# A decoder block on one Trainium2 core: accumulated values kept in the queries' tile, one group's sums moved to VectorE, one feed-forward's activations moved to ScalarE

## The chip, the cores and the metric

The kernel runs on one core of one Trainium2 chip. The metric is the device time of one launch, in microseconds (us). Before the change three runs gave 2163.33, 2163.65 and 2166.55 us, so the median is 2163.65 us.

The engines are named as the profile names them: PE is TensorE (PEld is its weight loads), DVE is VectorE, ACT is ScalarE, POOL is GpSimd, SP is SyncE, which issues most DMAs.

## The reference, cut to what matters

Four sequences of 1024 tokens and 512 features pass a self-attention with gates (phase 0), a cross-attention to a context of 384 features (phase 1), and a small feed-forward, each behind a layer norm and with a residual. Both attentions have 16 heads of 32. All data are 32-bit floats.

```python
q = (query @ Wq + bq).reshape(B, Nq, H, D).transpose(0, 2, 1, 3)
attn = softmax(q @ k^T * scale)            # cross-attention
x = x + (attn @ v) @ Wo + bo
s = layernorm(x) @ Win + bin_              # feed-forward: M = 64 units
h = relu(s[..., None] * W1 + b1)           # INNER = 16 activations per unit
g = sum_h(h * W2) + b2
out = x + g @ Wout + bout
```

What the change touches is in the cross-attention and the feed-forward: the softmax's denominator (a sum of exponentials over the keys), the division of attn @ v by it, and the 16 relus.

## The kernel before, in words

**Units and steps.** The work is eight *units*, (phase, sequence), in the list `order`; units 0 to 3 are the self-attention, 4 to 7 the cross-attention. Unit 7 is the *last unit*. A unit has two *halves* of 512 queries (`hf`), a half has four *groups* of four heads (`g`), and a group has eight *steps*, one per tile of 128 keys (`kt`). In one step of `attention(u, hf)`:

- `scores(g, kt)` (L615) multiplies keys and queries on PE (L623) into two PSUM tiles of two heads each, and ACT takes the exponential of each (L629) into a tile `e`. Six tiles `e` exist, three steps' worth. The PSUM tiles `s` are two; in the last unit, when no other work needs them (`spare`), the two banks `f` serve as a third (`score_banks`, L108).
- One step later `times` (L668) multiplies the values with `e` into the PSUM tile `av` (L671).

**The denominators.** Two ways are used. Where `shared` is false (units 4 to 6), DVE adds the exponentials of all four heads over the keys, two additions of 128x1024 per step (L646, L648). Where `shared` is true (phase 0 and the last unit), DVE adds those of the first two heads only, one addition per step, and PE sums the other two by multiplying with a column of ones (L679), four matmuls in every second step.

**The end of a group.** In the first step of the next group `normalize` (L685) copies `av` from PSUM with ACT into a tile `both` (L688) and, where `shared`, the sums `sm` too (L690). `both` has one buffer of three slots. One step later `add_up` (L698) sums the DVE partial sums over the partitions with a column of ones (L701), ACT copies that out (L702), and SP carries the sums through DRAM to a layout of 128x16 (L707 to L719). `divide` (L722) takes the reciprocals, and SP carries them through DRAM to all rows of a tile `recb` (L741, L745). `multiply` (L750) multiplies `both`'s first slot with `recb` into the queries' own tile `q` (L751), whose group is no longer needed as queries. `after(steps, f, behind)` holds such a part back by a number of steps; it then comes ahead of that step's scores, or behind them with `behind`. In the last unit the division is three steps after the sums, and the multiplication three steps after the division, ahead of the scores; in other units it is two steps, behind the scores.

**What runs beside.** `beside(u, hf)` lists what is put between the steps of a half, and `run` spreads it over them by its load. In the last unit that is, for the half before: the output projection (`project`, L106 called at L837), its residual and statistics on DVE (L845 to L850), the norm (L319) into tiles `r2` (two buffers), rows written to DRAM and read back turned (L323, L328), 32x32 transposes on DVE (L334), the feed-forward's first product (L937), the 16 hidden activations one by one (`hidden`, L982), and the output product into two PSUM banks `f` (L1011) with the residual on DVE (L1019). The hidden activations of a half are left over to the next half. Activation h is a relu with a scale and a bias per partition; the next call adds it, weighted, to `g` on DVE (L1000). The relu is on DVE (L989) for halves of units before the last, on ACT (L993) for the last unit's first half. Tile `hid` has two buffers, so activation h waits for the addition of activation h-2.

**Order.** The program writes each engine's instructions in the order of these calls, and each engine takes them in that order. The group that ends the kernel (`closing`) has its own sums and division (`settle`, L775).

Of the kernel before, what the change touches and what calls it, by code (L numbers as in the profile page):

```python
# [10 lines left out]
F32 = mybir.dt.float32  # L11
U32 = mybir.dt.uint32
AF = mybir.ActivationFunctionType
ALU = mybir.AluOpType
AX = mybir.AxisListType

P = 128
# [51 lines left out]
def moderate_path(tc: tile.TileContext, a: dict, out: bass.AP, flag: bass.AP):  # L69
    nc = tc.nc  # L70
    x = a["x"]
    with ExitStack() as st:
# [108 lines left out]
            raw.append(wp.tile([P, NC, D], F32, tag="w", name="w"))  # L181
            nc.sync.dma_start(raw[0], a["attn_Wout"].rearrange("(c p) f -> p c f", p=P))

        rot = p2.tile([P, NC, P], F32, tag="r2", name="rot")

        cs = p1.tile([P, 2, NC], F32, name="cs")
        gain = p1.tile([P, NC], F32, name="gain")
# [173 lines left out]
        def after(steps, f, behind=False):  # L361

            soon.append((tick[0] + steps, behind, f))
# [236 lines left out]
        def attention(u, hf):  # L600
# [3 lines left out]
            steps = []  # L604
            sums = 2 if ph == 0 else 1

            shared = ph == 0 or u + 1 == len(order)

            def apart(g):
                return 2 if u + 1 < len(order) else 3  # L610
# [1 line left out]
            def closing(g):  # L612
                return (u, hf, g) == (len(order) - 1, 1, HG - 1)

            def scores(g, kt):  # L615
                q, k = me["q", hf], me["k"]
                es = []
                for i in range(2):
                    two, reads = score_banks(not (closing(g) and kt == NT - 1))
                    for j in range(2):  # L620
                        r = slice((2 * i + j) * DH, (2 * i + j + 1) * DH)
                        for m in range(0, P, 64):
                            nc.tensor.matmul(  # L623
                                two[j][m : m + 64], lhsT=k[r, g, kt * P + m : kt * P + m + 64], rhs=q[r, g, :],
                                start=True, stop=True,
                            )
                    e = p4.tile([P, 2, HALF], F32, tag="e", name="e", bufs=6)
                    for h, s in reads:
                        nc.scalar.activation(e[:, h, :] if len(reads) == 1 else e[:, h.start, :], s, AF.Exp, scale=SCALE)  # L629
                    es.append(e)  # L630
                me["e", kt] = es
                if closing(g):
                    if kt == 0:
                        me["first"] = [p1.tile([P, 2, HALF], F32, tag=f"es{i}", name="es") for i in range(2)]
                    if kt in (0, 4, NT - 1):
                        return es
                    to = me["first"] if kt < 4 else me["rest"]
                    for i in range(2):
                        nc.vector.tensor_tensor(to[i], me["e", kt - 1][i] if kt % 4 == 1 else to[i], es[i], ALU.add)
                    if kt == 3:  # L640
                        after(2, lambda: by_ones(me["first"], True, False), behind=True)
                    return es
                for i in range(1 if shared else 2):
                    if kt == 1:
                        me.setdefault("es", {})[i] = p1.tile([P, 2, HALF], F32, tag=f"es{i}", name="es")
                        nc.vector.tensor_tensor(me["es"][i], me["e", 0][i], es[i], ALU.add)  # L646
                    elif kt > 1:
                        nc.vector.tensor_tensor(me["es"][i], me["es"][i], es[i], ALU.add)  # L648
                if ph == 0 and kt > 0:
                    if kt == 1:  # L650
                        me["eg"] = p1.tile([P, 2, HALF], F32, tag="es1", name="eg")
                    for h in range(2):
                        eg, gate = me["eg"][:, h, :], lambda t: me["sw"][:, t, HG * g + h, 1:2]
                        if kt == 1:
                            nc.scalar.activation(eg, me["e", 0][0][:, h, :], AF.Identity, scale=gate(0))  # L655
                        nc.vector.scalar_tensor_tensor(eg, es[0][:, h, :], gate(kt), eg, ALU.mult, ALU.add)  # L656
                return es
# [10 lines left out]
            def times(g, kt, es):  # L668
                for h in range(HG):
                    r = slice(h * DH, (h + 1) * DH)  # L670
                    nc.tensor.matmul(  # L671
                        av[r, :], lhsT=me["v"][:, kt, HG * g + h, :], rhs=es[h // 2][:, h % 2, :],
                        start=(kt == 0), stop=(kt == NT - 1),
                    )
                if shared and kt % 2 and not closing(g):

                    for j in range(4):
                        t, h = kt - 1 + j // 2, j % 2
                        nc.tensor.matmul(  # L679
                            sm[j * DH : j * DH + sums, :],  # L680
                            lhsT=me["sw"][:, t, HG * g + 2 + h, :] if ph == 0 else ones, rhs=me["e", t][1][:, h, :],
                            start=(kt == 1), stop=(kt == NT - 1),
                        )

            def normalize(g):  # L685
                i = (u * 2 + hf) * HG + g
                both = p1.tile([P, 3, HALF], F32, tag="both", name="both")
                nc.scalar.copy(both[:, 0, :], av)  # L688
                if shared:
                    nc.scalar.copy(both[:, 1, :], sm)  # L690
                    added = [me["es"][0][:, 0, :], me["es"][0][:, 1, :]]
                    if ph == 0:
                        added += [me["eg"][:, 0, :], me["eg"][:, 1, :]]
                else:
                    added = [me["es"][h // 2][:, h % 2, :] for h in range(HG)]
                after(1, lambda: add_up(g, i, both, added), behind=True)

            def add_up(g, i, both, added):  # L698

                for j, e in enumerate(added):  # L700
                    nc.tensor.matmul(sm[j * DH : j * DH + 1, :], lhsT=ones, rhs=e, start=True, stop=True)  # L701
                nc.scalar.copy(both[:, 2, :], sm)  # L702

                c, s1, s2 = cs_[i % 2], sum1_d[i % 4], sum2_d[i % 4]
                rows = both.rearrange("(j r) s q -> j r s q", r=DH)
                n = len(added)
                nc.sync.dma_start(s1[0:n], rows[0:n, 0, 2, :])  # L707
                if not shared:
                    nc.sync.dma_start(c[:, 0, 0, :], s1[0:n].rearrange("h (q e) -> (h q) e", e=INNER))
                else:  # L710
                    for k in range(sums):
                        nc.sync.dma_start(s2[k], rows[:, k, 1, :])
                    nc.sync.dma_start(
                        c[0:64, 0:sums, 0, :], s1[0:n].rearrange("(s h) (q e) -> (h q) s e", h=2, e=INNER)
                    )
                    for k in range(sums):
                        nc.sync.dma_start(
                            c[64:, k, :, :], s2[k].rearrange("(p h) (q e) -> (h q) p e", h=2, e=INNER)
                        )  # L719
                after(apart(g), lambda: divide(g, i, both, c))  # L720

            def divide(g, i, both, c):  # L722
                if shared:
                    both_ = p2.tile([P, sums, INNER], F32, tag="c2", name="both_")
                    nc.vector.tensor_tensor(both_, c[:, 0:sums, 0, :], c[:, 0:sums, 1, :], ALU.add)
                else:
                    both_ = c[:, 0:1, 0, :]
# [16 lines left out]
                for j in range(HG):  # L744
                    nc.sync.dma_start(  # L745
                        all_[j * DH : (j + 1) * DH, :], rec_d[i % 4][j : j + 1, :].to_broadcast([DH, HALF])
                    )
                after(apart(g), lambda: multiply(g, both, all_), behind=u + 1 < len(order))

            def multiply(g, both, all_):  # L750
                nc.vector.tensor_tensor(me["q", hf][:, g, :], both[:, 0, :], all_, ALU.mult)  # L751
                me["divided", hf] = g

            def step(g, kt):
# [20 lines left out]
        def settle(u, hf, g):  # L775
# [1 line left out]
            me = S[u]  # L777
            i = (u * 2 + hf) * HG + g
            rec = p1.tile([P, HALF], F32, tag="recb", name="recb")
            den = p1.tile([P, 3, HALF], F32, tag="both", name="den")[:, 0, :]  # L780
            few = p2.tile([P, INNER], F32, tag="rec", name="few")
            column = den.rearrange("p (b j) -> p b j", j=NB)[:, :, 0]

# [17 lines left out]
        def post(u, hf):  # L801
# [24 lines left out]
            def project(t):  # L826
                def part(cs, to=None):
                    def f():
# [20 lines left out]
                        nc.vector.bn_stats(s6, r)  # L849
                        nc.vector.bn_aggr(res["mv"][:, t, :], s6)  # L850
                        if ph == 0:
                            r2 = p2.tile([P, D], F32, tag="r2", name="r2")
                            nc.gpsimd.tensor_tensor(r2, r, bo_bc, ALU.add)  # L853
                            nc.sync.dma_start(x1b_d[b][4 * hf + t], r2)
                    return len(cs), f
# [45 lines left out]
            def norm(t):  # L901
                def f():
                    if last:
# [5 lines left out]
                        else:  # L909
                            normalized(to, res[t], res["mv"], res["rs", t], t)  # L910
                        return
                    r2 = p2.tile([P, 1, D], F32, tag="r2", name="r2")
                    normalized(r2[:, 0, :], res[t], res["mv"], res["rs", t], t)
                    away(rows_d[b][hf], r2, t, 1)
                return [(0, f)]
# [47 lines left out]

            def products():
                hid = res["hids"]
                both = p1.tile([P, 3, HALF], F32, tag="both", name="g")
                part, g = both[:, 0, 0 : 2 * P], both[:, 1, 0 : 2 * P]
                ph_ = bank()[:, 0 : 2 * P]
                on_pe = sorted(res["diag"], key=lambda h: (h - BY_ACT) * 1.25 if h >= BY_ACT else h * 1.6 + 0.5)
# [12 lines left out]
            def hidden(h):  # L982
                def f():

                    own = u + 1 < n
                    if h < INNER:
                        hid = p2.tile([P, 2 * P], F32, tag="hid", name="hid")
                    if own and h < INNER:
# [880 lines left out]
```

## Time and profile before

| what | value |
|---|---|
| runs | 2163.33, 2163.65, 2166.55 us; median 2163.65 us |
| profiled execution | 2166.25 us, of which the span from first to last instruction is 2164.4 us |
| instructions | 52976 |
| mean granted PE clock | 0.998 |
| last unit's first half, groups 0 to 3 start at | 1916.24, 1939.89, 1972.88, 1993.95 us |
| last unit's second half, groups 0 to 3 start at | 2018.08, 2042.58, 2075.57, 2096.64 us |
| ACT L629, exponential of 128x1024 | 1023 ns each |
| DVE L648, addition of 128x1024 | 1227 ns each |
| DVE L989 and ACT L993, relu of 128x256 | 409 ns and 605 ns each |
| DVE L751, the multiplication of 128x512 | 686 ns each |

A matmul of 32-bit floats appears as two records in the trace, so four matmuls side by side are eight. Four records on the four column groups of the array take about 0.43 us to issue; a record's own duration (592 ns) contains the drain, which overlaps what follows. A step's length is therefore read from the start of one step's scores to the start of the next. In the profile's tables "idle before" is the idle time of an engine just before an instruction, and the arrow names what ended it. "PEclk" is the granted share of PE's full clock.

### The profile page before, as it was taken

The page shows a single profiled execution, that of the slowest core. Times are in us where ns is not written, and L with a number is a line of the kernel's source. Part 1 is how long each engine was busy: PE and PEld are TensorE (multiplying, and loading weights), DVE is VectorE, ACT ScalarE, POOL GpSimd, SP SyncE. Part 2 cuts the span into 40 slices and gives each one's busy share as a digit, 9 for nine tenths or more (in the row PEclk, how much of TensorE's full clock was granted, in tenths as well). Part 3 has the DMA queues.
Part 4 walks back from the last instruction along what each step waited for, and adds up shares of the span by engine and source line. Part 5 has one row for each costly group of instructions (what it writes and reads, how often), then busy time and mean ns, then how long its engine had stood idle before and what let it go on. Part 6 is the DMA issues. An engine that isn't in the chain of part 4 may idle for free.

```text
span 2164.4 us, 52976 instructions
## 1 busy us (share of the span) xinstructions
PE 2145.8 (99%) x22792; PEld 555.9 (26%) x22792; DVE 1503.4 (69%) x2251; ACT 1233.1 (57%) x1495; POOL 133.0 (6%) x182
## 2 busy tenths in 40 slices
PE   9999999999999999999999999999999999999998
PEld 4322222222222222222222222222222222222223
DVE  3477675786766866657667666787878868876656
ACT  0156545655556554565666666565655566566765
POOL 2000010040120100001000010000000000000001
PEclk9999999999999999999999999999999999999999
DMA  6412134032331221211322113322423122322231
GB/s 169 122 47 68 52 100 114 19 87 69 90 109 34 81 59 53 68 48 65 71 71 79 63 59 69 96 66 71 89 80 102 63 61 57 98 60 71 71 90 47
DMA packets 154136, 161.71 MB, mean 75 GB/s; under 512 B 47002, under 2 KB 92698, under 8 KB 152740
## 3 DMA queue, kind: packets, MB, share of 16 engines
q1 hardware_dynamic: 149828, 156.14, 25.9%
q8 instruction: 180, 2.95, 0.6%
q0 software_dynamic: 2080, 0.98, 0.3%
q10 hardware_dynamic: 1984, 1.12, 0.2%
q14 instruction: 64, 0.52, 0.1%
HBM read 115.40 MB, written 42.74 MB: 73 GB/s over the span
## 4 chain that ended last, share of the span: by engine, by line
PE 97%; DVE 1%; ACT 1%; issue 1%; DMA 0%; SPq 0%; POOL 0%; DVEq 0%; ACTq 0%
PE f L106 37%; PE s L623 24%; PE av L671 23%; PE sm L679 6%; PE sm L701 3%; PE s L106 1%; PE f L937 1%; ACT e L629 1%; PE f L623 0%; PE f L1011 0%; DMA xin<-in_x 0%; PE f L498 0%; DVE res L1019 0%; PE f L971 0%; DVE es L648 0%
## 5 line engine op out<-in xcount | busy, mean ns | idle before, releaser
L629 ACT ACTIVATE e<-s 128x1024 f32<-128x1024 f32 x997 | 969.4, 1023 | 715.7 <-PE s L623 509.1
L648 DVE TENSOR_TENSOR es<-es,e 128x1024 f32<-128x1024 f32 x522 | 628.4, 1227 | 259.2 <-ACT e L629 258.4
L623 PE MATMUL s<-q,k 32*64 32x512 f32 x7976 | 583.6, 613 | 0.5 <-ACT e L629 0.4
L671 PE MATMUL av<-e,v 128*32 128x512 f32 x4096 | 551.6, 604 | 0.0
L106 PE MATMUL f<-xT,w 128*32 128x512 f32 x2816 | 333.7, 592 | 0.0
L656 DVE SCALAR_TENSOR_TENSOR eg<-e,sw,eg 128x512 f32<-128x512 f32 x448 | 315.6, 746 | 9.3 <-ACT eg L655 9.3
L646 DVE TENSOR_TENSOR es<-e 128x1024 f32<-128x1024 f32 x87 | 104.4, 1223 | 213.4 <-ACT e L629 202.6
L106 PE MATMUL f<-w,q 128*32 128x512 f32 x1984 | 238.6, 593 | 2.0 <-DVE res L845 1.8
L623 PEld LDWEIGHTS s<-q,k 32*64 32x64 f32 x7976 | 127.0, 129 | 412.4 <-ACT e L629 201.6
L671 PEld LDWEIGHTS av<-e,v 128*32 128x32 f32 x4096 | 88.4, 108 | 403.4 <-issue 403.0
L106 PEld LDWEIGHTS f<-xT,w 128*32 128x32 f32 x2816 | 92.2, 110 | 210.4 <-issue 208.0
L679 PE MATMUL sm<-e,sw 128*2 128x512 f32 x1024 | 133.3, 592 | 0.0
L106 PE MATMUL f<-w,xT 128*32 128x512 f32 x896 | 106.0, 592 | 0.6 <-DVE q L308 0.6
L106 PEld LDWEIGHTS f<-w,q 128*32 128x32 f32 x1984 | 64.9, 110 | 152.1 <-issue 143.2
L106 PE MATMUL f<-w,ctxT 128*32 128x512 f32 x768 | 92.3, 592 | 0.0
L106 PE MATMUL f<-ctxT,w 128*32 128x512 f32 x768 | 92.3, 592 | 0.0
L853 POOL TENSOR_TENSOR r<-res,bo_bc 128x512 f32<-128x512 f32 x32 | 40.9, 1278 | 759.4 <-DVE res L845 613.2
L701 PE MATMUL sm<-es,fixed 128*1 128x512 f32 x348 | 66.1, 596 | 3.5 <-ACT both L690 3.3
L314 POOL TENSOR_SCALAR rs<-fmv 128x4 f32<-128x4 f32 (+2 forms) x18 | 10.1, 562 | 854.8 <-DVE fmv L850 854.8
L845 DVE TENSOR_TENSOR res<-f,res 128x512 f32<-128x512 f32 x62 | 42.6, 687 | 27.7 <-PE f L106 15.0
L1000 DVE SCALAR_TENSOR_TENSOR g<-hid,units,g 128x256 f32<-128x256 f32 x105 | 50.3, 479 | 0.9 <-ACT hid L993 0.2
L751 DVE TENSOR_TENSOR q<-both,recb 128x512 f32<-128x512 f32 x63 | 43.2, 686 | 8.5 <-DMA recb<-rec_d 8.5
(285 smaller groups left out, 1185.6 us busy)
## 6 DMA issues: line engine op xcount, KB each, us to landing
recb<-rec_d SPq DMA_DIRECT2D x252, 64.0 KB
xT<-rows_d SPq DMA_DIRECT2D x60, 256.0 KB
rows_d<-r SPq DMA_DIRECT2D x60, 256.0 KB
w<-in_xattn_Wo SPq DMA_DIRECT2D x9, 1024.0 KB
w<-wout_d SPq DMA_DIRECT2D x8, 1024.0 KB
res<-in_x SPq DMA_DIRECT2D x32, 256.0 KB
x1b_d<-r SPq DMA_DIRECT2D x32, 256.0 KB
res<-x1b_d SPq DMA_DIRECT2D x32, 256.0 KB
```

The costliest lines, as they stand in the source:

```text
L106: nc.tensor.matmul(to[r], lhsT=lhsT[:, j, :] if len(lhsT.shape) == 3 else lhsT[:, r], rhs=rhs, **flags)
L623: nc.tensor.matmul(two[j][m : m + 64], lhsT=k[r, g, kt * P + m : kt * P + m + 64], rhs=q[r, g, :], start=True, stop=True,)
L629: nc.scalar.activation(e[:, h, :] if len(reads) == 1 else e[:, h.start, :], s, AF.Exp, scale=SCALE)
L646: nc.vector.tensor_tensor(me["es"][i], me["e", 0][i], es[i], ALU.add)
L648: nc.vector.tensor_tensor(me["es"][i], me["es"][i], es[i], ALU.add)
L656: nc.vector.scalar_tensor_tensor(eg, es[0][:, h, :], gate(kt), eg, ALU.mult, ALU.add)
L671: nc.tensor.matmul(av[r, :], lhsT=me["v"][:, kt, HG * g + h, :], rhs=es[h // 2][:, h % 2, :], start=(kt == 0), stop=(kt == NT - 1),)
L679: nc.tensor.matmul(sm[j * DH : j * DH + sums, :], lhsT=me["sw"][:, t, HG * g + 2 + h, :] if ph == 0 else ones, rhs=me["e", t][1][:, h, :], ...
L701: nc.tensor.matmul(sm[j * DH : j * DH + 1, :], lhsT=ones, rhs=e, start=True, stop=True)
L751: nc.vector.tensor_tensor(me["q", hf][:, g, :], both[:, 0, :], all_, ALU.mult)
L845: nc.vector.tensor_tensor(r, res["po"], r, ALU.add)
L1000: nc.vector.scalar_tensor_tensor(res["g"], res["hid"], units[:, 2, h - 1 : h], res["g"], ALU.mult, ALU.add)
```

## The change

1. `normalize` copies `av` straight into the queries' tile, `me["q", hf][:, g, :]`, and `multiply` multiplies there in place. `both` loses the slot that held the values and has two.
2. `shared` becomes a function of the group: in the last unit group 1 of each half is no longer shared. DVE sums all four heads there, and PE's L679 falls away for that group.
3. The relus of unit 6's first half (computed beside the last unit's first half) go to ACT; the bias terms follow.
4. `multiply` comes behind the scores of its step in the last unit too, and one step later for groups 0 and 1.
5. `r2` has three buffers.

```diff
-        rot = p2.tile([P, NC, P], F32, tag="r2", name="rot")
+        rot = p2.tile([P, NC, P], F32, tag="r2", name="rot", bufs=3)
...
-            shared = ph == 0 or u + 1 == len(order)
+            def shared(g):
+                return ph == 0 or (u + 1 == len(order) and not (g == 1))
...
-                for i in range(1 if shared else 2):
+                for i in range(1 if shared(g) else 2):
...
-                if shared and kt % 2 and not closing(g):
+                if shared(g) and kt % 2 and not closing(g):
...
-                both = p1.tile([P, 3, HALF], F32, tag="both", name="both")
-                nc.scalar.copy(both[:, 0, :], av)
-                if shared:
-                    nc.scalar.copy(both[:, 1, :], sm)
+                both = p1.tile([P, 2, HALF], F32, tag="both", name="both")
+                nc.scalar.copy(me["q", hf][:, g, :], av)
+                if shared(g):
+                    nc.scalar.copy(both[:, 0, :], sm)
...
-                nc.scalar.copy(both[:, 2, :], sm)
+                nc.scalar.copy(both[:, 1, :], sm)
...
-                after(apart(g), lambda: multiply(g, both, all_), behind=u + 1 < len(order))
+                after(apart(g) + (u + 1 == len(order) and g < 2), lambda: multiply(g, all_), behind=True)
 
-            def multiply(g, both, all_):
-                nc.vector.tensor_tensor(me["q", hf][:, g, :], both[:, 0, :], all_, ALU.mult)
+            def multiply(g, all_):
+                own = me["q", hf][:, g, :]
+                nc.vector.tensor_tensor(own, own, all_, ALU.mult)
                 me["divided", hf] = g
...
-                            r2 = p2.tile([P, D], F32, tag="r2", name="r2")
+                            r2 = p2.tile([P, D], F32, tag="r2", name="r2", bufs=3)
...
-                    own = u + 1 < n
+                    own = u + 1 < n and (u, hf) != (n - 2, 0)
```

The remaining lines renumber the slots of `both` in the DMAs and in the two other places that borrow the tile, call `shared(g)` in `divide` and `add_up`, and give the third buffer to the norm's `r2`. The names and lines in this document are those of the kernel before; in the changed kernel they lie one to three lines further on.

More of the change, by code (lines that the diff above doesn't have):

```diff
@@ L706, in add_up @@
                 n = len(added)
-                nc.sync.dma_start(s1[0:n], rows[0:n, 0, 2, :])
-                if not shared:
+                nc.sync.dma_start(s1[0:n], rows[0:n, 0, 1, :])
+                if not shared(g):
                     nc.sync.dma_start(c[:, 0, 0, :], s1[0:n].rearrange("h (q e) -> (h q) e", e=INNER))
@@ L711, in add_up @@
                     for k in range(sums):
-                        nc.sync.dma_start(s2[k], rows[:, k, 1, :])
+                        nc.sync.dma_start(s2[k], rows[:, k, 0, :])
                     nc.sync.dma_start(
@@ L719, in add_up, with divide @@
                         )
-                after(apart(g), lambda: divide(g, i, both, c))
-            def divide(g, i, both, c):
-                if shared:
+                after(apart(g), lambda: divide(g, i, c))
+            def divide(g, i, c):
+                if shared(g):
                     both_ = p2.tile([P, sums, INNER], F32, tag="c2", name="both_")
@@ L779, in settle @@
             rec = p1.tile([P, HALF], F32, tag="recb", name="recb")
-            den = p1.tile([P, 3, HALF], F32, tag="both", name="den")[:, 0, :]
+            den = p1.tile([P, 2, HALF], F32, tag="both", name="den")[:, 0, :]
             few = p2.tile([P, INNER], F32, tag="rec", name="few")
@@ L911, in f @@
                         return
-                    r2 = p2.tile([P, 1, D], F32, tag="r2", name="r2")
+                    r2 = p2.tile([P, 1, D], F32, tag="r2", name="r2", bufs=3)
                     normalized(r2[:, 0, :], res[t], res["mv"], res["rs", t], t)
@@ L965, in products @@
                 hid = res["hids"]
-                both = p1.tile([P, 3, HALF], F32, tag="both", name="g")
+                both = p1.tile([P, 2, HALF], F32, tag="both", name="g")
                 part, g = both[:, 0, 0 : 2 * P], both[:, 1, 0 : 2 * P]
```

## The prediction

> **What bounds the kernel now.** I read the page's busy times, then its chain of work, then PE's waits.
>
> ```profile
> PE 2145.8 (99%) x22792; PEld 555.9 (26%) x22792; DVE 1503.4 (69%) x2251; ACT 1233.1 (57%) x1495; POOL 133.0 (6%) x182
> ...
> PE 97%; DVE 1%; ACT 1%; issue 1%; DMA 0%; SPq 0%; POOL 0%; DVEq 0%; ACTq 0%
> ```
> ```profile
> PE sm L701 <- ACT both L690: 3.3, 2, 2.1
> PE f L106 <- DVE res L845: 1.8, 1, 1.8
> ```
>
> PE is the bound everywhere. So an edit counts by the PE work that it takes away, by the PE waits that it ends, and by those that it makes. The largest wait (total, times, longest) is of the sums' matmul for ScalarE's copy: 1.24 us in the last unit's first half, 2.05 us in its second. The timeline of the second shows the chain:
>
> ```profile
> 2100.91 0.69 DVE L751 TENSOR_TENSOR q<-both,recb 128x512 f32<-128x512 f32 x1 [1.70 <-DMA recb<-rec_d]
> ...
> 2101.68 0.59 ACT L688 COPY both<-av 128x512 f32<-128x512 f32 x1 [1.88 <-PE s L623]
> 2102.16 0.59 ACT L690 COPY both<-sm 128x512 f32<-128x512 f32 x1
> ...
> 2102.88 1.02 PE L701 MATMUL sm<-es,fixed 128*1 128x512 f32 x2 [2.05 <-ACT both L690]
> ```
>
> The multiplication of group 1 waited for a DMA; the copies of group 2 need its tile `both`, start when it ends at 2101.60 (the profile names an older PE event), and PE waits for them. The stages around it, by windows (PE, PEld, DVE, ACT and POOL busy, then PEclk), show a second cost:
>
> ```profile
> 2102.00:2103.00 1.00, 0.12 (x4) 0.15 (x8) 1.00 (x2) 1.00 (x3) 0.00 (x0) 0.94 0.00 0
> 2103.00:2106.30 3.30, 3.30 (x20) 0.78 (x20) 1.80 (x3) 2.19 (x3) 0.00 (x0) 0.50 0.00 0
> 2106.30:2109.00 2.70, 2.70 (x46) 1.10 (x42) 0.92 (x1) 0.72 (x2) 0.00 (x0) 1.00 0.03 6
> ```
>
> PE got half its clock for some 3.4 us after that wait: 1.7 us lost. The waits of 1.24 us (1999) and 1.82 us (1611) are followed by no such drop.
>
> **What goes.** *PE's sums of group 1.* Steps with and without them, from the start of one step's scores to the next:
>
> ```profile
> 1953.69 1.11 PE L623 MATMUL s<-q,k 32*64 32x512 f32 x16
> ...
> 1957.45 1.11 PE L623 MATMUL s<-q,k 32*64 32x512 f32 x16
> 1958.49 1.06 PE L671 MATMUL av<-e,v 128*32 128x512 f32 x8
> 1959.38 1.04 PE L679 MATMUL sm<-e,fixed 128*1 128x512 f32 x8
> 1960.23 1.90 PE L106 MATMUL f<-w,q 128*32 128x512 f32 x16
> 1962.06 1.11 PE L623 MATMUL s<-q,k 32*64 32x512 f32 x16
> ```
>
> 3.76 us without, 4.61 us with: 0.86 us each. Four in each half go: 8 x 0.86 = **6.9 us**. The sums over the partitions (L701) become four matmuls for two. Four of them with the values' eight records lasted from 1919.48 to the next scores at 1921.31, 1.83 us; two from 1976.99 to 1978.81, 1.82 us: 0. One copy of `sm` on ScalarE and two DMAs per half go too; nothing waits for these.
>
> *The copies' wait.* `av` now goes into the queries, whose last reader is PE a step earlier, and `both`'s readers are DMAs long landed. The copies can start when ScalarE is free, at 1997.10 instead of 1998.17 and at 2099.80 instead of 2101.68. The sums' matmul then finds the copy done about 0.15 us late (this is what the same place costs at 1976.99). 1.24 + 2.05 - 0.3 = **3.0 us**. Next late there is VectorE's last addition (ended 2102.74). It now stands ahead of the multiplication, but behind three transposes that wait for rows read back. In the second half these came 20.2 us after the output residuals (2077.10 to 2097.31); the third `r2` buffer ends one 0.5 us norm's wait in between; then 1.8 for the transposes and 1.2 for the addition: 22.7 us. PE asks 22.3 us after group 2's second step begins (2078.49 to 2099.72, and 1.05), which is when the residuals end in the sum below. **0.3 us** late, up to 1.5. In the first half the same sum is 18.9 + 3.0 = 21.9 against 22.3: 0.
>
> *The clock*: **1.7 us**, in executions that have the drop.
>
> [...]
>
> **What comes.** *VectorE in group 1.* Seven additions more per half, each 1227 ns; in a row they start 1.13 us apart:
>
> ```profile
> 1612.16 4.60 DVE L648 TENSOR_TENSOR es<-es,e 128x1024 f32<-128x1024 f32 x4
> ```
>
> (4.60 - 1.22)/3. Busy before in group 1's window: 22.6 of 33.0 us in the first half, 17.0 of 33.0 in the second. After: 22.6 + 8.6 - 3.0 (hidden activations moved) = 28 and 25.6, of 33.0 - 3.4 = 29.6. That fits, but the end does not. From the start of step 5, second half: exponentials are ready 2.21 us after a step's start (1962.06 to 1964.27); two additions 2.26; residual and statistics 1.55; two additions of step 6 2.26, output residuals 1.20, two of step 7 2.26, output residuals 1.20 and 0.08 to their end: 13.0 us. They free the two banks `f` that group 2's second step wants for scores; PE is there after 3.76 + 3.10 + 3.10 + 2.06 = 12.0 us. PE waits **1.0 us**, part of it earlier, where the second output product wants the first one's banks. In the first half one weighted addition (0.39) and a start 0.46 late come on top: **1.9 us**. I take these; each can be 0 (additions that fall into gaps) or twice.
>
> *Relus on ScalarE.* 16 at 0.49 us from start to start (2113.42 to the exponential at 2113.91) are 7.8 us. ScalarE is busy 17.3 of 23.7 us in group 0 and 17.0 of 33.0 in group 1, so 9 and 7 of them fit. VectorE loses 16 x 0.41. Going through the queue step by step from the rows, ScalarE falls at most 0.6 us behind, one score tile comes late: **0.3 us**; 0 to 2.
>
> *The multiplication behind the scores.* In the second half, step 7 of group 0:
>
> ```profile
> 2040.75 1.90 PE L106 MATMUL f<-w,q 128*32 128x512 f32 x16
> 2041.03 1.22 DVE L648 TENSOR_TENSOR es<-es,e 128x1024 f32<-128x1024 f32 x1 [1.06 <-ACT e L629]
> ```
>
> Before, the last group's multiplication ran at 2039.29, ahead of this addition. Now the addition is first (it needs step 7's exponential), the multiplication follows at 2042.16 and ends at 2042.85. The second eight of PE's records are the projection's last quarter, which reads its product; they started at 2041.61 and now wait till 2042.9: **1.3 us**. Behind PE's wait are only the next step's scores. Groups 0 and 1 have a step more, and nobody reads them before the next half; group 2 of the second half comes where VectorE has no addition, so 0.
>
> *At nothing*: the multiplication in place (same form, 686 ns); the third `r2` buffer, which ends up to 4.2 us of VectorE's waits for DMA in a stretch where PE waits for other things; units 0 to 6, where instructions keep their order.
>
> **The sum.** Gone 6.9 + 3.0 = 9.9, come 0.3 + 1.0 + 1.9 + 0.3 + 1.3 = 4.8: 5.1 us, and 6.8 us with the clock. The profiled execution took 2166.25 us (span 2164.4 and 1.85 around it): 2166.25 - 6.8 = 2159.4, a span of 2157.6. It lies 2.6 us over the median of the runs, 2163.65. If the median runs don't have the clock's drop, they go to 2158.5; if they do, to 2156.9. I predict **2158.0 us**, nearer to the first: a profiled execution so far above the median is the likelier one to hold the drop.
>
> **The rivals.** *VectorE keeps up* (its additions fall into gaps, or PE's waits overlap): 2.9 us of waits go, the rest stays: 2158.5 - 2.9 = 2155.6 us, with the clock 2153.9. For it: 1.6 to 4.0 us are free by the sums of group 1. Against: step 5's exponentials set the start of the chain, so earlier gaps don't help.
>
> *VectorE's backlog doubles*: 2.9 more, and 2158.5 + 2.9 = 2161.4; if the waits of the first half (1.1 and 0.7 us, within 3.4 us of each other) halve the clock as 2.05 us did, 1.7 more, 2163.1. Against: 1.82 us at 1611 did not.
>
> *Slower: ScalarE becomes the bound in the first half.* A relu waits for a buffer that VectorE frees behind two additions; ScalarE's exponentials stand behind the relu, and PE behind these. The three such waits in the trace took 4.6 us: 0.24, 0.34 and 4.0. If group 0's nine relus had no cover (4.4 us) and group 1's two places with two relus in a row each waited 4.0, PE would lose 12.4 us instead of 0.3: 2158 + 12.1 = 2170 us. It decides once a step's exponentials and relus (1.94 + 0.49 to 0.98, and the wait) exceed PE's step; steps of group 0 last 2.04 and 3.06 alternately, 2.55 on average against 2.43, so the margin there is 0.1 us; in group 1 it is over 1 us.
>
> *It doesn't do what it says*: excluded; the order of instructions in the changed program has eight rows of L679 fewer.
>
> **How the numbers follow.** Chances: the forecast 0.48 (2156.0 to 2159.3), VectorE keeps up 0.22, backlog doubles or a wait I priced at 0 shows 0.21 (2159.3 to 2164), slower 0.09. About 0.2%, 4.3 us, is what a measurement of this kernel can tell from no change. Faster by more 0.70, within 0.21, slower 0.09. The range for 8 in 10 goes from the first rival with the clock to the middle of the second: 2153.5 to 2162.5.
>
> **What would show it.** Right: no wait of L701 over 0.3 us in groups 2 to 3, no half clock in mid-kernel, group 1's steps of 3.76 throughout, waits of PE for L1019 near the end of group 1 (two per half) and for L751 in the second half's group 0. Wrong: PE waiting for exponentials between 1916 and 1975, waits over 2 us, or L701 waiting for L648.

## The result, and the profile after

The changed kernel takes 2158.49 us, the median of eight runs (2157.87 to 2159.57). The kernel before took 2163.70 us in eight runs (2163.33 to 2166.55). The ratio is 0.997, 95% interval 0.9961 to 0.9979: about 0.3% faster, 0.5 us above the forecast of 2158.0 us. The profiled execution took 2158.01 us, with a span of 2156.2 us.

The page's busy times after, then PE's waits (total, times, longest):

```profile
PE 2139.9 (99%) x22736; PEld 554.1 (26%) x22736; DVE 1512.7 (70%) x2247; ACT 1239.1 (57%) x1509; POOL 136.2 (6%) x182
```
```profile
...
PE f L106 <- DVE q L753: 1.1, 1, 1.1
PE f L106 <- DVE q L308: 1.1, 2, 0.6
PE f L106 <- DVE res L847: 1.1, 1, 1.1
PE f L1013 <- DVE res L1021: 0.6, 1, 0.6
...
```

PE is still the bound. The largest wait of before, of the sums' matmul for ScalarE's copy, is gone. Two are new: L753 is the multiplication (L751 before), L1021 the output residual (L1019 before).

Lengths from the starts of steps show where the time went. Units 0 to 4 and 6 agree to 0.01 us in every half. Unit 5's second half is 0.72 us shorter, which is not put down to the change: the half holds PE's wait for the residual addition (L845 before, L847 after; 1.8 and 1.1 us), whose rows are loaded just ahead of it, and it took 121.98 to 123.11 us in the fourteen profiles of this study, 122.40 to 123.02 in the kernel before alone. The last unit, in us:

| step | before | after | what |
|---|---|---|---|
| first half, whole | 101.84 | 99.24 | |
| group 1, steps 2 and 4, in both halves | 4.62 | 3.76 | PE's sums gone |
| group 0, steps 4 and 7 | 3.06, 3.76 | 3.12, 3.91 | relus on ScalarE |
| group 1 steps 6 and 7, group 2 steps 0 and 1 | 3.96, 3.10, 2.92, 3.01 | 3.47, 4.39, 2.04, 3.24 | sums gone, VectorE's queue late |
| group 3, step 1 | 5.90 | 4.64 | the copies' wait gone |
| second half, to VectorE's last instruction | 139.69 | 134.77 | |
| group 0, step 7 | 3.76 | 5.09 | the multiplication behind |
| group 1 steps 6 and 7, group 2 steps 0 and 1 | 3.96, 3.10, 2.92, 3.01 | 3.10, 3.81, 2.04, 3.23 | as in the first half |
| group 3, step 1 | 8.38 | 4.64 | wait and half clock gone |

Together 7.52 us, 5.8 without the half clock. The other two of the four sums that go in each half lay in step 6 of group 1 and step 0 of group 2, in the rows with VectorE's queue. What follows VectorE's last instruction took 6.6 us before and 6.4 after.

The place of the wait that went, second half, after (timelines of VectorE, ScalarE and PE: start, duration, engine, line, operation; the idle time before it and what ended that in brackets):

```profile
2092.20 1.90 DVE L334 STREAM_TRANSPOSE xn<-xn 128x512 f32<-128x512 f32 x3 [1.47 <-DMA xn<-rows_d]
2094.02 1.18 DVE L649 TENSOR_TENSOR es<-es,e 128x1024 f32<-128x1024 f32 x1
2095.12 0.70 DVE L334 STREAM_TRANSPOSE xn<-xn 128x512 f32<-128x512 f32 x1
2096.06 0.69 DVE L753 TENSOR_TENSOR q<-q,recb 128x512 f32<-128x512 f32 x1 [0.23 <-DMA recb<-rec_d]
```
```profile
2095.43 0.61 ACT L689 COPY q<-av 128x512 f32<-128x512 f32 x1
2095.89 0.63 ACT L691 COPY both<-sm 128x512 f32<-128x512 f32 x1
```
```profile
2095.48 1.11 PE L624 MATMUL s<-q,k 32*64 32x512 f32 x16
2096.58 0.60 PE L702 MATMUL sm<-es,fixed 128*1 128x512 f32 x2
```

The copies no longer follow the multiplication; they start before it. VectorE's addition ends at 2095.20, and PE comes to L702 at 2096.58 with both ready: no wait, and 1.38 us to spare on VectorE's side.

The two new waits. Second half, group 0, step 7, on PE and on VectorE:

```profile
2037.69 1.04 PE L106 MATMUL f<-w,q 128*32 128x512 f32 x8
2039.86 1.07 PE L106 MATMUL f<-w,q 128*32 128x512 f32 x8 [1.12 <-DVE q L753]
```
```profile
2037.98 1.22 DVE L649 TENSOR_TENSOR es<-es,e 128x1024 f32<-128x1024 f32 x1 [1.66 <-ACT e L630]
2039.12 0.68 DVE L753 TENSOR_TENSOR q<-q,recb 128x512 f32<-128x512 f32 x1
```

The projection's last eight records stand still until the multiplication, now behind the addition, has ended. And the end of group 1 in the first half:

```profile
1967.09 2.33 DVE L649 TENSOR_TENSOR es<-es,e 128x1024 f32<-128x1024 f32 x2
1969.33 1.28 DVE L1021 TENSOR_TENSOR res<-f,res 128x512 f32<-128x512 f32 x2
1970.53 2.35 DVE L649 TENSOR_TENSOR es<-es,e 128x1024 f32<-128x1024 f32 x2
1972.80 1.28 DVE L1021 TENSOR_TENSOR res<-f,res 128x512 f32<-128x512 f32 x2
1974.00 0.68 DVE L753 TENSOR_TENSOR q<-q,recb 128x512 f32<-128x512 f32 x1
```
```profile
1970.07 1.72 PE L1013 MATMUL f<-wout,g 64*128 64x512 f32 x4 [0.63 <-DVE res L1021]
1971.72 1.11 PE L624 MATMUL s<-q,k 32*64 32x512 f32 x16
1972.77 1.06 PE L672 MATMUL av<-e,v 128*32 128x512 f32 x8
1973.76 1.02 PE L624 MATMUL f<-q,k 32*64 32x512 f32 x4
```

VectorE is busy without a gap. The second output product waits for the first one's residuals, and group 2's second scores (1973.76) start in the banks `f` as the last residuals free them. In the second half the profile names no such wait; the cost shows in step 7 of group 1, 3.81 us for 3.10.

### The profile page after: what moved, and what is told of

Its sections match the earlier page's. It is cut to its first block, busy times and chain, and to the rows that moved or that the text cites. A ratio compares the mean times of both kernels' runs of the same rounds, so it can differ in the third digit from the quotient of the medians.

```text
span 2156.2 us, 52835 instructions
## 1 busy us (share of the span) xinstructions
PE 2139.9 (99%) x22736; PEld 554.1 (26%) x22736; DVE 1512.7 (70%) x2247; ACT 1239.1 (57%) x1509; POOL 136.2 (6%) x182
## 4 chain that ended last, share of the span: by engine, by line
PE 96%; DVE 2%; ACT 1%; issue 1%; DMA 0%; SPq 0%; POOL 0%; DVEq 0%; ACTq 0%
PE f L106 37%; PE s L624 24%; PE av L672 22%; PE sm L680 6%; PE sm L702 3%; PE s L106 1%; PE f L939 1%; ACT e L630 1%; DVE es L649 1%; PE f L624 1%; PE f L1013 0%; DMA xin<-in_x 0%; PE f L498 0%; DVE res L1021 0%; PE f L973 0%
## 5 line engine op out<-in xcount | busy, mean ns | idle before, releaser
L649 DVE TENSOR_TENSOR es<-es,e 128x1024 f32<-128x1024 f32 x534 | 641.4, 1225 | 255.7 <-ACT e L630 254.6
L702 PE MATMUL sm<-es,fixed 128*1 128x512 f32 x356 | 65.3, 591 | 0.0
L847 DVE TENSOR_TENSOR res<-f,res 128x512 f32<-128x512 f32 x62 | 42.4, 684 | 24.1 <-PE f L106 18.2
L680 PEld LDWEIGHTS sm<-e,sw 128*2 128x2 f32 x1024 | 26.9, 85 | 79.8 <-issue 79.8
```

Source lines behind the costliest of these rows:

```text
L680: nc.tensor.matmul(sm[j * DH : j * DH + sums, :], lhsT=me["sw"][:, t, HG * g + 2 + h, :] if ph == 0 else ones, rhs=me["e", t][1][:, h, :], ...
L847: nc.vector.tensor_tensor(r, res["po"], r, ALU.add)
```

## The experiments

The times are compared with runs of the kernel before on the same chip, whose medians were 2165.16, 2164.70 and 2164.21 us (33, 17 and 21 runs, 2162.99 to 2168.20 in all). "The wait" is that of the sums' matmul in group 3; a step there takes 4.64 us without it.

### The parts alone

**The values' copy alone.** Only the copy into the queries' tile, and the multiplication there in place; the sums, the relus, the time of the multiplication and two buffers `r2` as before.

```diff
-                nc.scalar.copy(both[:, 0, :], av)
+                nc.scalar.copy(me["q", hf][:, g, :], av)
```

> The kernel before with the values copied into the queries' tile and multiplied there, and nothing else: the multiplication stays ahead of the scores, three steps after the division. Theory: two things come late for PE at the sums over the partitions in groups 2 to 3, the copies of av and sm and VectorE's last addition, which stands behind the multiplication and so behind the same DMA (it ended 2102.74 us, the matmul started 2102.88). With the copies free the matmul waits for the addition: 1.24 and 2.05 us become about 1.15 and 1.95, and the time falls by 0.2 us, 2163.5. Rival: each part counts for itself; the wait is of the tile alone, 3.0 us go, and the clock's drop with them: 2160.6 or less.

Measured: 2163.85 us, ratio 0.9995 (0.9986 to 1.0004); span 2161.4 us. The waits stay, 1.17 and 1.37 us. The second half, on VectorE, then on PE:

```profile
2099.18 0.69 DVE L753 TENSOR_TENSOR q<-q,recb 128x512 f32<-128x512 f32 x1 [1.64 <-DMA recb<-rec_d]
2099.79 1.22 DVE L649 TENSOR_TENSOR es<-es,e 128x1024 f32<-128x1024 f32 x1
```
```profile
2101.15 0.60 PE L702 MATMUL sm<-es,fixed 128*1 128x512 f32 x2 [1.37 <-DVE es L649]
```

The copies were done, but VectorE's addition stood behind a multiplication that waited for its DMA. That is the wait "next late" of the prediction, and the theory held in kind (it had 1.15 and 1.95 us). The first half has the same order: the multiplication starts at 1996.35, the addition ends at 1998.18, and the matmul starts at 1998.33; there the profile names an exponential that ended beside the addition.

**The later multiplication alone.**

```diff
-                after(apart(g), lambda: multiply(g, both, all_), behind=u + 1 < len(order))
+                after(apart(g) + (u + 1 == len(order) and g < 2), lambda: multiply(g, both, all_), behind=True)
```

> The kernel before with the multiplication behind the scores and a step later for groups 0 and 1 of the last unit, and nothing else; the tile with three slots stays. Theory: the copies still wait for the multiplication of group 1, which still waits for its DMA, so the waits of 1.24 and 2.05 us stay or grow to 2.5 (the addition is now ahead of the multiplication), and the second half's step 7 of group 0 gains the wait of 1.3 us for the last group's product: 2165 us. Rival: the later place alone ends the waits, 2161 to 2162 us.

Measured: 2166.48 us, ratio 1.0006 (0.9997 to 1.0015); span 2162.8 us. The waits are 1.13 and 1.60 us, both still for the copies, and step 7 of the second half's group 0 takes 5.09 us for 3.76. So this part alone pays its price and gains nothing that the times show, as the theory had it. The profiled execution, 2164.60 us, was the fastest of its eleven; how long the waits are in the slower ones no trace shows.

**Both together, without the moved sums and relus**, and the third buffer `r2` with it:

```diff
-                return ph == 0 or (u + 1 == len(order) and not (g == 1))
+                return ph == 0 or (u + 1 == len(order) and True)
...
-                    own = u + 1 < n and (u, hf) != (n - 2, 0)
+                    own = u + 1 < n
```

> The changed kernel without the moved sums and without the moved relus: the values copied into the queries' tile, the later multiplication and the third buffer r2 are left. Theory: the values' copy alone and the later multiplication alone each left one of two queues in front of the sums' matmul (VectorE's addition behind the multiplication; the copies behind the multiplication), so together they take both waits away: the steps with the wait go from 5.90 and 8.38 us to about 4.64 in both halves, no half clock in mid-kernel, and step 7 of the second half's group 0 is 1.33 us longer. Span: 2164.4 - 1.26 - 3.74 + 1.33 = 2160.7 us. Rival: it is the two DMAs fewer and the earlier copy that come with the moved sums which end the waits (sums alone ended the first one); then some 1.2 us of wait stay in each half, as with the values alone, and the span is about 2163.1.

Measured: 2162.97 us, ratio 0.9992 (0.9983 to 1.0001). Both steps take 4.64 us: no wait is left. VectorE in the second half, then PE:

```profile
2099.03 1.18 DVE L649 TENSOR_TENSOR es<-es,e 128x1024 f32<-128x1024 f32 x1
2100.13 0.70 DVE L334 STREAM_TRANSPOSE xn<-xn 128x512 f32<-128x512 f32 x1
2100.75 0.65 DVE L753 TENSOR_TENSOR q<-q,recb 128x512 f32<-128x512 f32 x1
```
```profile
2101.29 0.60 PE L702 MATMUL sm<-es,fixed 128*1 128x512 f32 x2
```

The theory held: two queues stood in front of one matmul, each part clears one, and neither is enough by itself. The steps show this; the interval of the times still reaches 1. The span, 2161.6 us, is 0.9 over the expected one; the last unit took 237.88 us to VectorE's last instruction, 3.65 less than before where the theory's steps give 1.26 + 3.74 - 1.33 = 3.67. The rest lies outside these steps: 0.29 us at the start, 0.09 in unit 5 and 0.44 behind VectorE's last instruction.

**The same with two buffers `r2`.**

The tile of the norm, and likewise the two others with this tag:

```diff
...
-                    r2 = p2.tile([P, 1, D], F32, tag="r2", name="r2", bufs=3)
+                    r2 = p2.tile([P, 1, D], F32, tag="r2", name="r2")
```

> As the kernel with the values' copy and the later multiplication, but r2 with two buffers. Theory: the rows read back come later by the norm's wait for its buffer, VectorE's transposes hold its addition back, and the sums' matmul waits for that addition as in the changed kernel with two buffers (1.60 us) or with the values alone (1.37 us), in the second half alone: 1 to 1.6 us over the kernel with three buffers, span about 2162. Rival: without the moved sums VectorE reaches the norms earlier by about 0.9 us, so the wait is below 0.5 us and the two kernels are alike.

Measured: 2162.86 us, ratio 0.9992 (0.9983 to 1.0001); both steps 4.64 us. The theory fell, the rival held: without the moved sums the third buffer does nothing.

**The sums of group 1 alone.**

```diff
-            shared = ph == 0 or u + 1 == len(order)
+            def shared(g):
+                return ph == 0 or (u + 1 == len(order) and not (g == 1))
...
```

> The kernel before with group 1 of the last unit summed on VectorE for all four heads, and nothing else: the relus stay on VectorE, the values go through the tile with three slots. 6.9 us of PE work go. Theory: VectorE's queue at the end of group 1 costs PE 1.0 us in the second half and 1.9 plus some 2.3 (seven relus of 0.32 us more) in the first; PE then stands that much nearer to the DMA chain that follows the output residuals, so the waits at group 3's second step grow by 1.4 us each, with the clock's drop in one or both: 2163.7 - 6.9 + 5.2 + 2.8 = 2164.8, up to 2167 with the drops. Rival: each part counts for itself: 2163.7 - 6.9 + 2.9 = 2159.7.

Measured: 2160.35 us (2158.84 to 2166.06), ratio 0.9984 (0.9975 to 0.9993). My theory fell, the rival was near. I had the copies' waits grow behind VectorE's longer queue; but the first half's is gone (step 4.64 us) and the second's is 1.75 us, with no half clock. The reciprocals of group 1 came back at 1994.58, and the sums' matmul was not due before 1997.32. Group 1 now sends two DMAs fewer per half, but that alone doesn't explain it: SP issued the reciprocals' first DMA 13.14 us after group 2's start in the first half, for 15.82 before, and in the second half, with two fewer as well, 16.09 us for 16.21. What brought them early in the first half stays open. Four of the eleven runs took 2162.78 to 2166.06 us, three of them at a lower granted clock (0.997, 0.998 and 0.997, for 0.999 in the other eight); no trace shows what they waited for.

The queue at the end of group 1 costs more than in the changed kernel. Step 7 is the same (4.39 and 3.81 us), but steps 0 and 1 of group 2 take 2.42 and 3.46 us in both halves, for 2.04 and 3.24. The multiplication of group 0 (0.60 us, at 1970.93) still stands between the residuals of the two output products; in the changed kernel it comes behind them (1974.00). So the later place, which costs 1.33 us in the second half's group 0, also takes 0.6 us off this queue in each half.

### The changed kernel with one part undone or improved

**The relus back on VectorE** (the line of `own` as before).

> The changed kernel with the relus of unit 6's first half back on VectorE. Theory: seven of them fall in group 1 of the last unit's first half, where VectorE is the late one, and lengthen its queue by 7 x 0.32 = 2.3 us; ScalarE's 0.2 us of late score tiles go. PE's waits at the two output products and at group 2's second step, 1.9 us together, become some 4: 2158.5 + 2.1 = 2160.6, and 1.7 more where the clock halves. Rival: VectorE has slack there and the relus on ScalarE cost what they save: 2158.3.

Measured: 2159.19 us, ratio 0.9971 (0.9960 to 0.9983). The theory fell: the first half takes 99.29 us for 99.24. Most of the seven relus of group 1 fall into VectorE's gaps, since its additions wait for exponentials (1.76 and 1.05 us there in the changed kernel). The move takes 0.26 us off step 6 of group 1 and puts 0.2 on group 0: worth 0.05 us.

**Two buffers `r2` in the changed kernel** (the three tiles with this tag, as above).

> The changed kernel with two buffers for r2. Theory: VectorE waits some 2 us for the rows' DMA in group 2 of the second half, the rows come back up to 0.5 us later, and PE's matmul at group 3's second step, for which VectorE's addition was ready in time, waits 0 to 0.5 us: 2158.5 to 2159.0. Rival: the third buffer carries part of the gain (over 1 us).

Measured: 2161.01 us, ratio 0.9982 (0.9973 to 0.9992). VectorE in the second half, then PE:

```profile
2082.35 1.18 DVE L319 TENSOR_SCALAR r<-res,fmv,rs 128x512 f32<-128x512 f32 x2 [4.57 <-DMA rows_d<-r]
...
2095.01 1.90 DVE L334 STREAM_TRANSPOSE xn<-xn 128x512 f32<-128x512 f32 x3 [3.04 <-DMA xn<-rows_d]
2096.84 1.18 DVE L649 TENSOR_TENSOR es<-es,e 128x1024 f32<-128x1024 f32 x1
```
```profile
2098.17 0.60 PE L702 MATMUL sm<-es,fixed 128*1 128x512 f32 x2 [1.60 <-DVE es L649]
```

The norm waits 4.57 us for its buffer, the rows read back come at 2095.01 instead of 2092.20, and the transposes hold the addition back until PE waits 1.60 us. The theory fell, the rival held. So the third buffer is worth 1.6 us, but only beside the moved sums. With them VectorE begins the norms 2.87 us after group 2's start, for 2.05 in the version above with two buffers, and PE comes to group 3 sooner, 20.42 us after that start for 21.07; these two make up some 1.5 us, and the rest is in how long the rows take.

**The multiplication ahead again where PE needs it**, that is for groups 2 and 3:

```diff
-                after(apart(g) + (u + 1 == len(order) and g < 2), lambda: multiply(g, all_), behind=True)
+                after(apart(g) + (u + 1 == len(order) and g < 2), lambda: multiply(g, all_), behind=u + 1 < len(order) or g < 2)
```

> The changed kernel with the multiplication of groups 2 and 3 in the last unit ahead of the scores again (groups 0 and 1 stay behind). Theory: the second half's step 7 of group 0 loses its wait of 1.1 us for the product (5.09 us become 3.76), nothing else moves: 2158.5 - 1.3 = 2157.2. Rival: the wait is of something else that comes at the same time, such as the DMA of the reciprocals; then the step stays at 5.1 and the time at 2158.5.

Measured: 2157.85 us (2157.17 to 2160.42), ratio 0.9965 (0.9952 to 0.9979). Step 7 of group 0 is back to 3.76 us, the second half takes 133.45 us for 134.77, and nothing else moves. The theory held. By the steps it is 1.3 us better than the changed kernel. Its median of five runs is the lowest here, but only 0.6 us lower, in another batch of runs, and both profiles have a span of 2156.2 us: the start, units 5 and 6 and what follows VectorE's last instruction were together 1.3 us longer in this one. So the times alone don't show the gain.

**The output products later**, on top of that:

```diff
-                out += pause(2) + weave(h[0:k], pause(10)) + weave(h[k:] + (ending[0]["prep"] if hf else []), last["o"]) + held.pop()["out"]
-                out += (ending[0]["load"] if hf else []) + weave(last["ln"], pause(5)) + last["xT"]
+                out += pause(2) + weave(h[0:k], pause(10)) + weave(h[k:] + (ending[0]["prep"] if hf else []), last["o"])
+                out += (ending[0]["load"] if hf else []) + weave(last["ln"], pause(5)) + last["xT"] + held.pop()["out"]
```

> The version with the product ahead, and in the last unit the two output products of the held feed-forward put behind the norms instead of ahead of them, so that they fall in group 2, where VectorE has time. Theory: the waits at the output products and at group 2's second step (1.9 us in the first half, 0.9 in the second) go: 2157.2 - 2.8 = 2154.4, if nothing in group 2 waits in their place (ScalarE is near its bound there: a step of 2.04 us against 2.0). Rival: the waits are of VectorE's sum over the whole of groups 1 and 2 and only move: 2157.2.

Measured: 2158.53 us, ratio 0.9969 (0.9957 to 0.9981). The waits at the end of group 1 went, and came back where the products now stand: step 1 of the first half's group 2 takes 5.29 us for 3.24, and the halves take 100.04 and 133.90 us where the version without this edit had 99.24 and 133.45. They only moved, as the rival had it.

### The half clock

**The kernel before, three more profiles.**

> The kernel before, unchanged, for a second profile and more times. Its times so far lie in two clumps, near 2163.6 and near 2166.4 us. Theory: the upper clump is the executions in which PE's clock halves for 3.4 us after the wait of 2.05 us; then a profile with a span near 2161.7 us shows no half clock in mid-kernel, and one near 2164.4 us shows it. Rival: the clumps have another cause (transfers at the start or at 1611 us); then the half clock is there in both, or in neither.

> The kernel before, unchanged, one more look. [...]

> [...] With the half clock about 2166 us; without it about 2164.2 us.

Measured: 2165.82, 2166.35 and 2164.71 us in the profiled executions. The first one was also timed: 2164.59 us, ratio 0.9998 (0.9989 to 1.0007). The second half's wait in the second and third of these, and the windows behind it (PE, PEld, DVE, ACT and POOL busy, then PEclk):

```profile
2103.15 0.60 PE L701 MATMUL sm<-es,fixed 128*1 128x512 f32 x2 [2.33 <-ACT both L690]
```
```profile
2104.50:2107.80 3.30, 3.30 (x30) 1.28 (x26) 2.13 (x2) 0.84 (x2) 0.00 (x0) 0.50 0.01 4
```
```profile
2102.83 0.60 PE L701 MATMUL sm<-es,fixed 128*1 128x512 f32 x2 [1.69 <-ACT both L690]
```
```profile
2104.50:2107.80 3.30, 3.30 (x50) 1.32 (x50) 1.82 (x2) 1.77 (x5) 0.00 (x0) 1.00 0.03 9
```

The same program, and in the last of the four profiles the step takes 6.35 us instead of 8.38, 8.60 and 8.67. So the half clock isn't in every execution. Where it is missing the wait is also the shortest, 1.69 us for 2.05, 2.25 and 2.33. The wait itself varies, with the DMA that brings the reciprocals (the multiplication starts 4.47, 4.54 and 3.90 us after group 3 in these three, 4.27 in the first profile).

How often it occurs can be read from the mean granted clock of each run. It is 0.998 in the three profiles with the half clock and 0.999 in the one without. Of the 82 timed runs of the kernel before in these experiments 28 have 0.998 or less, of the changed kernel's eight none. So about two executions in three lack it. The count is rough, since the mean doesn't say where the clock fell: one of the runs with the relus back has 0.998 from a half clock at 9.59 us.

## Why the prediction was right

Without the half clock it had 5.1 us, where the steps give 5.8. Its mechanism held, but for the third `r2` buffer; that the time came within 0.5 us of the forecast is in part luck, since the forecast stood between two estimates 1.6 us apart and the medians differ by 0.6 us less than the steps. Its terms, in us:

| term | predicted | measured | by |
|---|---|---|---|
| PE's sums of group 1 | 6.9 gone | 6.9 gone | 4.62 to 3.76 in four steps; the other four taken as the same |
| the copies' waits, less 0.3 | 3.0 gone | 3.3 gone | 5.90 to 4.64; 2.05 of 8.38 to 4.64 |
| VectorE's addition late | 0.3 come | 0 | step 4.64 in both halves |
| queue at the end of group 1, first and second half | 1.9, 1.0 come | 1.89, 0.93 come | 0.37 + 1.29 + 0.23; 0.71 + 0.22 |
| relus on ScalarE | 0.3 come | 0.21 come | group 0, steps 4 and 7 |
| the multiplication behind | 1.3 come | 1.33 come | 3.76 to 5.09 |
| half clock | 1.7 gone, where it occurs | 1.7 gone | 3.74 less the wait of 2.05 |

- *The sums and the two costs on VectorE and PE* held within 0.1 us, by the queue written out from the rows. The versions that undo or take alone one part give the same steps: 5.09 with the later multiplication alone, 3.76 when it goes ahead; 4.39 and 3.81 with the sums alone. That the queue holds no multiplication is due to the later place: with the sums alone it does, and costs 0.6 us more in each half.
- *The copies' wait* went, by 0.3 us more than forecast, since the allowance of 0.15 us per half wasn't needed. In the first half it is ended twice over: the sums alone end it too. That the addition behind the transposes is next late was right, and its 0.3 us was 1.7 too cautious: it had 1.38 us to spare in the second half. The transposes' rows came 17.9 us after the residuals (2074.34 to 2092.20), for an assumed 20.2 - 0.5 = 19.7.
- *The third `r2` buffer at nothing* is the step that failed. The prediction credited it with 0.5 us of a norm's wait and otherwise put it where PE waits for other things. It ends 2.8 us of the rows' way (2095.01 to 2092.20), and without it PE waits 1.60 us. In the sum this error did no harm, because the changed kernel has the buffer.
- *The relus* were priced right as a cost, 0.21 us. The relief of VectorE that they bring was taken into the first half's queue as well; it is 0.26 us, and the move is worth nothing.
- *The rivals.* VectorE did not keep up, nor was its backlog double; PE's wait for exponentials is 0.4 us in the whole kernel, so ScalarE isn't the bound. The third rival misread the rows of the first half's group 0: its steps don't alternate between 2.04 and 3.06 us but last 2.04, 3.03, 2.90, 2.04, 3.06, 2.04, 4.78 and 3.76, 2.96 on average, so the margin there was wider than 0.1 us. Of the signs that the prediction named, the waits for L1019 came in part: the profile names one, in the first half.
- *The choice between the medians.* The runs' medians differ by 5.2 us, nearer to the 5.8 without the half clock than to the 7.5 with it. By the granted clocks 54 of 82 runs of the kernel before lack it, so the estimate that the prediction leaned to was the right one. In the profile without it the last unit took 239.58 us to VectorE's last instruction, 5.57 more than the 234.01 of the changed kernel: the wait itself is shorter there, 1.69 us for 2.05.

## What to carry to other kernels

When two engines' queues lead to one waiting matmul, find both before pricing either edit: alone, neither the values' copy nor the later multiplication moved the time measurably, and together they end both waits, 3.3 us in the profile before. An instruction put behind another on its engine is to be priced at every place where it runs: of its seven places in the last unit one cost 1.33 us, where PE needs the product in the same step, and two took 0.6 us each off VectorE's queue once the sums had moved. A buffer's worth depends on which engine is late: nothing without the moved sums, 1.6 us with them.

## What the runs showed of the hardware

PE's granted clock was 0.50 behind the sums' matmul's waits of 2.05 and 2.33 us, by the windows above. Behind that of 2.25 us the second pair of L701 took 1.07 us, as behind the 2.05 (1.07) and not as behind the 1.69 (0.60). In the profile before the clock stayed at half for 3.41 us (2102.87 to 2106.28). No half clock followed the waits of 1.60, 1.60, 1.69 and 1.75 us at the same place in four other profiles, whose mean clock is 0.999, nor the wait of 1.82 us at 1611 in the profile before. The half clock began at the end of the wait in one execution (2102.87 against 2102.88) and 1.3 us behind it in another (2104.45 against 2103.15). With the relus back, one began at 9.59 us, behind two waits of which the longer took 1.70 us. So the length of a single wait doesn't settle it in these runs, and what does was not shown.
